# Post-norm block on one core: the later order of the maxima begins at step 20, with the quantizing in the middle of the step

## The chip, the cores and the metric

The kernel runs on one core of one Trainium2 chip. The metric is the device time of one execution in microseconds. The engines are TensorE (PE, with its weight loads as PEld), VectorE (DVE), ScalarE (ACT), GpSimd (POOL) and SyncE (SP), which here only issues DMAs.

## The reference, cut to what matters

For four sequences of 512 rows of width 512: attention with 16 heads of width 32 that share one key and one value head, rotary positions, a residual sum and a layer norm; then a gated feed-forward net with three weights that are first quantized to -1, 0 and 1, again a residual sum and a layer norm.

```python
q = rotary((x @ Wq + bq) by heads);  k = rotary(x @ Wk + bk);  v = x @ Wv + bv
attn = softmax(q @ k.T / sqrt(32));  ctx = attn @ v
x = layernorm(x + ctx @ Wo + bo)
quantize = lambda w: clip(round(w / (mean(abs(w)) + 1e-8)), -1, 1)
hidden = sigmoid(x @ quantize(w1).T) * (x @ quantize(w2).T)     # width 1408
x = layernorm(x + hidden @ quantize(w3).T)
```

## The kernel before, in words

**Steps.** The main loop (`for n, (b, c, t) in enumerate(steps)`, from line 865 on) has 64 steps: batch `b` of 4, group `c` of 4 heads, key chunk `t` of 4 (128 keys each). A step computes the scores of its four heads against its key chunk (`scores`: tiles `ps`, two exponentials `es`), and multiplies the previous step's exponentials with the values (`weigh`: `acc`). For batch 0 `count` also sums them into the PSUM bank `den`; for later batches POOL adds them up (`total`, four additions in each step but the first of a group), and `normalize` turns these into a divisor in several parts (`part`, `few`, `rden`).

**Maxima.** The scores need the row maxima beforehand. `find_maxima(n + 7, ...)` computes those of one head of a later group, seven steps ahead, in chunks of 128 queries: a matmul into `pmax` by PE and a reduce `maxima<-pmax` by DVE. `maximum` (line 379) says where `pmax` lies. PSUM has eight banks: two score buffers of two banks each (`ps_sc`), which the scores and the maxima use in turn, `acc` and `den` of one bank and one buffer each (`ps_acc`), and two buffers of one bank for all other products (`ps_mm`). A call with two chunks takes a score buffer. A call with one chunk takes `den` if it is chunk 0, or if `batches[-1].done == NC`, which is when the last batch's queries have been projected; otherwise a score buffer. With a head's last chunk in a group, `spread` (line 394) is entered in the list `late` three due times on: it transposes the group's maxima (`pm`, `m`) and sends them through DRAM (`rows`) into the tile `negm` that the scores take.

**Fill.** All other work of PE is cut into pieces and drawn between: `project_in` (keys, values and queries of a batch: `pk`, `pq`, with the rotation by four DVE operations), `project_out` (`po<-wo_sb`, then sum, statistics and layer norm on `xt`, then transposes `pt` and their two halves `y`), `feed_forward` (`gu`, `po<-wd`). `Fill.draw(us, least)` adds `us` to what is due and takes pieces, each counted at the length that it yields, while more than 0.9 is due; with `least` it takes one in any case. `Fill.one` changes between an urgent and an ordinary list. A step of batch 1 has a pace of 3.8. When nothing can be taken, what is due is set to zero.

**Due times.** `due` counts `slot` up, twice per step, and carries one part of each entry of `late` whose time has come (parts of `normalize`, `spread`, `layernorm`, storing of queries, and others).

**Quantizing.** `quantized` (line 158) has 66 jobs: three weights by eleven tiles, each tile read once for the mean and once to be quantized. A job of the second kind is a sign on ACT into `sgn`, a `scalar_tensor_tensor` on DVE (`raw<-raw,hi,sgn`), and two DMAs that POOL issues (`raw<-in_wf` for a later job, `w<-raw` for an earlier one). From step 17 on `sgn` lies in the tag `rot_a`, which has one buffer (line 210). 21 jobs are done ahead of step 0, two in each step of batch 0; from step 16 on one in each step and two where `n % 3 == 0`, so that the 66th falls in step 25. Steps 20 to 25 hold the last eight.

**Order.** `InOrder`, `mm`, `move` and `transpose` (lines 70 to 86) keep each engine's instructions in the order in which the program states them, so lines 75, 80, 83 and 86 stand for nearly all instructions in the profile, and tiles tell them apart. The order of a step of batch 1 is one of two, chosen at line 886. With the last batch not yet projected: maxima of chunk 0, of chunks 1 and 2, of chunk 3; first due time; one quantizing job; the whole draw; a second job where there is one; second due time. Otherwise: chunk 0; a draw of 0.4 of the pace; chunks 1 and 2; first due time; a draw of 0.3 with `least`; chunk 3; a draw of 0.3; second due time, and no quantizing.

Of the kernel before, what the change touches and what calls it, by code (L numbers as in the profile page):

```python
# [28 lines left out]
def postln_block(  # L29
# [17 lines left out]
    NC = D // P  # L47
    NT = T // P
# [30 lines left out]
    def mm(out, lhsT, rhs, start, stop):  # L79
        pin(nc.tensor.matmul(out, lhsT=lhsT, rhs=rhs, start=start, stop=stop))  # L80
# [36 lines left out]
    batches = [Batch() for _ in range(B)]  # L117

    chunks = iter([(b, c) for b in range(B) for c in range(NC)])
# [226 lines left out]
    def load_q(b, c):  # L346
        q = batches[b].q[c] = work.tile([P, T], F32, tag="qT", name="qT", bufs=3)
        move(q, batches[b].qd[c][0])
# [15 lines left out]
    def room_for_maxima(b, c):  # L364

        return maxima[c % 2][:, 0 : NG * NT].rearrange("p (i t) -> p i t", t=NT)
# [12 lines left out]
    def maximum(b, c, i, chunks, q):  # L379


        s = batches[b]
        if i == 0 and chunks[0] == 0:
            s.mx[c] = room_for_maxima(b, c)
        if len(chunks) == 1 and (chunks[0] == 0 or batches[-1].done == NC):
            ps = ps_acc.tile([P, 1, T], F32, tag="den", name="pmax")
        else:
            ps = ps_sc.tile([P, 2, T], F32, tag="sc", name="pmax")
        ps = ps[:, 0 : len(chunks), :]
        for n, t in enumerate(chunks):  # L390
            mm(ps[:, n, :], q[:, ts(t, P)], s.kr, True, True)
        dve.tensor_reduce(s.mx[c][:, i, chunks[0] : chunks[-1] + 1], ps, AX.X, ALU.max)
# [21 lines left out]
    def scores(b, c, t):  # L414
        s = batches[b]
        pss = []
        for j in range(2):
            ps = ps_sc.tile([P, 2, T], F32, tag="sc", name="ps")
            pss.append(ps)
            for i in range(2):  # L420
                rows = ts(2 * j + i, HD)
                mm(ps[:, i, :], s.kT[rows, ts(t, P)], s.q[c][rows, :], True, False)
        for j, ps in enumerate(pss):
            for i in range(2):
                rows = slice(HD * (2 * j + i), HD * (2 * j + i) + 2)
                mm(ps[:, i, :], ones_r[rows, :], s.negm[c][rows, :], False, True)
        es = []
        for j, ps in enumerate(pss):
            e = esp.tile([P, 2, T], F32, tag="es", name="es")
            act.activation(e, ps, AF.Exp, scale=SCALE)  # L430
            es.append(e)
        if b > 0:

            if t == 0:
                s.first = es
            elif t == 1:
                s.total = [work.tile([P, 2, T], F32, tag=f"total{j}", name="total", bufs=1) for j in range(2)]
                for j in range(2):
                    for i in range(2):
                        pool.tensor_tensor(  # L440
                            s.total[j][:, i, :], s.first[j][:, i, :], es[j][:, i, :], ALU.add
                        )
            else:
                for j in range(2):
                    for i in range(2):
                        pool.tensor_tensor(
                            s.total[j][:, i, :], s.total[j][:, i, :], es[j][:, i, :], ALU.add
                        )
        return es
# [5 lines left out]
    def weigh(b, c, t, es):  # L455
        s = batches[b]
        if t == 0:
            s.acc = ps_acc.tile([P, T], F32, tag="acc", name="acc")
            s.ctxT[c] = work.tile([P, T], F32, tag="ctxT", name="ctxT", bufs=6)
        columns(s.acc, s.v[:, t, :], es, t == 0, t == NT - 1)  # L460
        if t == NT - 1:
            act.copy(s.ctxT[c], s.acc)

    def count(b, c, t, es):

        s = batches[b]
        if t == 0:
            s.den = ps_acc.tile([P, T], F32, tag="den", name="den")
        columns(s.den, ones[:, 0:HD], es, t == 0, t == NT - 1)
# [95 lines left out]
    def load_x(b):  # L565
        batches[b].x = []
        for t in range(NT):
            xt = xp.tile([P, D], F32, tag="x", name="xt")
            move(xt, x[b, ts(t, P), :])
            batches[b].x.append(xt)  # L570
        yield
        for xt in batches[b].x:
            pool.tensor_tensor(xt, xt, bo_sb, ALU.add)
            yield
# [212 lines left out]
    def quantize(n):  # L787
        for _ in range(n):
            next(weights, None)

    steps = [(b, c, t) for b in range(B) for c in range(NC) for t in range(NT)]
    PER = NC * NT
# [5 lines left out]
    now = -1  # L798
# [3 lines left out]
    def due():  # L802

        nonlocal slot
        slot += 1
        for entry in list(late):
            if slot >= entry[0] and next(entry[1], "end") == "end":
                late.remove(entry)

    def begin_middle():  # L810
        late.extend(middle)
        middle.clear()
# [9 lines left out]
    def find_maxima(k, *chunks):  # L822

        if k >= len(steps):
            return
        b, c, i = steps[k]
        if chunks[0] == 0:
            ask(k + HEADS)
            while batches[b].done <= c or (b and k not in heads):
                if batches[b].done <= c:  # L830
                    fill.one()
                else:
                    begin_middle()
                    due()
                    ask(k)
        if b == 0:
            row_maxima(b, c, i, chunks[0] // 2)
        else:
            maximum(b, c, i, chunks, heads[k])
        if i == NG - 1 and chunks[-1] == NT - 1:  # L840

            late.insert(0, (slot + (1 if now < 0 else 3), spread(b, c)))

    def feed(b):
        fill.urgent.append(project_out(b))
        yield
# [18 lines left out]
    for n, (b, c, t) in enumerate(steps):  # L865
        now = n
        pace = (1.8, 3.8, 4.8, 4.6)[b]
        if t == 1 and PER <= n + NT - 1 < len(steps):
            load_q(*steps[n + NT - 1][:2])
        es = scores(b, c, t)  # L870
        if last is not None:
            weigh(*last)
        if last is not None and last[0] == 0:
            count(*last)
        last = (b, c, t, es)
        if n == NC * NT // 2:

            late.append((slot, load_x(0)))
        if t == NT - 1:
            begin = slot + 3  # L880
            late.append((begin, normalize(b, c)))
            if c == NC - 1:
                late.append((begin + 7, feed(b)))
                if b > 0:
                    late.append((slot + 6, load_x(b)))
        if batches[-1].done < NC:

            if b == 0:
                find_maxima(n + LEAD, 0, 1)
                begin_middle()  # L890
                due()
                find_maxima(n + LEAD, 2, 3)
            else:
                find_maxima(n + LEAD, 0)
                find_maxima(n + LEAD, 1, 2)
                find_maxima(n + LEAD, 3)
                begin_middle()
                due()
            quantize(1)
            fill.draw(pace)  # L900
            quantize(1 if b == 0 or n % 3 == 0 else 0)
        else:
            find_maxima(n + LEAD, 0)
            fill.draw(0.4 * pace)
            find_maxima(n + LEAD, 1, 2)
            begin_middle()
            due()
            fill.draw(0.3 * pace, True)
            find_maxima(n + LEAD, 3)
            fill.draw(0.3 * pace)  # L910
        due()
    weigh(*last)
    now = len(steps)
# [68 lines left out]
```

## Time and profile before

| what | value |
| --- | --- |
| median of 3 runs | 661.32 us (660.82 to 663.54) |
| the profiled execution | 659.87 us |
| its span, first to last instruction | 658.1 us |
| granted TensorE clock, mean | 0.997 |
| steps 20 to 25, by the starts of their scores | 179.94 to 223.97 us |
| DVE busy in steps 20 to 24 | 7.20 of 7.33, 7.35 of 7.42, 6.95 of 7.33, 6.66 of 7.32, 7.71 of 8.98 us |
| POOL busy in the same | 7.31, 6.64, 6.88, 6.54, 6.75 us |

A row of a timeline reads: start, length, engine, line, operation, tile written and tiles read, shapes, how many were merged into the row, and in brackets the idle time of the engine before it and what ended it. A `q` behind an engine's name is its queue of DMAs. A row of the windows reads: stretch, its length, busy time of each engine with the number of instructions, granted clock, share of the DMA engines, GB/s.

### The profile page before, as it was taken

What the parts mean: (1) busy time and instruction counts of PE and PEld (TensorE: products, weight loads), DVE (VectorE), ACT (ScalarE), POOL (GpSimd) and SP (SyncE); (2) the same over time, 40 slices, a digit from 0 to 9 for tenths busy, and PEclk for the clock granted to TensorE, in tenths of its full rate; (3) what the DMA queues carried; (4) which work ended last, traced back from release to release, by engine and by line L of the source; (5) the groups of instructions that cost most, each with busy time, mean ns of one, the idle gap of its engine ahead of it and who ended that gap; (6) DMA issues with size and microseconds to landing.
All of it is one profiled execution on the core that took longest, in us unless ns stands there. A gap on an engine that the chain in (4) does not pass through costs nothing.

```text
span 658.1 us, 9358 instructions
## 1 busy us (share of the span) xinstructions
PE 635.4 (97%) x3194; PEld 357.2 (54%) x3194; DVE 440.3 (67%) x629; ACT 282.6 (43%) x441; POOL 327.4 (50%) x416
## 2 busy tenths in 40 slices
PE   8999999999999999999999899999998999999995
PEld 5233333443333356665555566655555685778884
DVE  3987765787998977676666867667536544364335
ACT  2474656564454645333244354333454521234213
POOL 2434344545998766467666275576575703202000
PEclk9999999999999999999999999999999999999998
DMA  8946669788676286464132457541131473237531
GB/s 265 316 164 209 204 194 273 230 254 259 171 238 205 89 250 190 136 191 147 46 106 77 117 163 219 158 143 44 55 116 52 145 236 120 81 112 229 175 109 64
DMA packets 60671, 107.78 MB, mean 164 GB/s; under 512 B 14592, under 2 KB 15360, under 8 KB 60624
## 3 DMA queue, kind: packets, MB, share of 16 engines
q1 hardware_dynamic: 51984, 80.57, 40.2%
q0 software_dynamic: 7920, 25.96, 12.3%
q10 hardware_dynamic: 720, 0.66, 0.4%
q8 instruction: 25, 0.41, 0.3%
q14 instruction: 22, 0.18, 0.1%
HBM read 84.06 MB, written 23.10 MB: 163 GB/s over the span
## 4 chain that ended last, share of the span: by engine, by line
PE 85%; DVE 9%; ACT 4%; issue 2%; POOL 0%; DVEq 0%; ACTq 0%; POOLq 0%
PE gu L80 24%; PE po L80 19%; PE ps L80 13%; PE pmax L80 9%; PE acc L80 7%; PE pq L80 7%; DVE maxima L75 3%; ACT es L75 2%; PE den L80 2%; PE pk L80 2%; DVE part L75 1%; DVE xt L75 1%; DVE y L75 1%; DVE st L75 1%; PE warm L80 1%
## 5 line engine op out<-in xcount | busy, mean ns | idle before, releaser
L75 DVE TENSOR_REDUCE maxima<-pmax 128x1 f32<-128x512 f32 (+1 forms) x169 | 157.8, 955 | 69.9 <-PE pmax L80 69.7
L75 ACT ACTIVATE es<-ps 128x1024 f32<-128x1024 f32 x128 | 124.2, 1021 | 117.6 <-PE ps L80 116.7
L80 PE MATMUL gu<-y,wg 128*128 128x512 f32 x704 | 171.6, 393 | 0.1
L80 PEld LDWEIGHTS gu<-y,wg 128*128 128x128 f32 x704 | 131.7, 188 | 33.7 <-issue 4.9
L75 POOL TENSOR_TENSOR total<-total,es 128x512 f32<-128x512 f32 x96 | 125.2, 1336 | 38.5 <-ACT es L75 38.3
L80 PE MATMUL po<-wd,h 128*128 128x512 f32 x352 | 86.5, 394 | 3.3 <-DVE y L75 2.9
L75 POOL TENSOR_TENSOR total<-es 128x512 f32<-128x512 f32 x48 | 60.9, 1302 | 52.5 <-ACT es L75 52.5
L80 PE MATMUL pmax<-kr,qr 128*128 128x512 f32 x192 | 74.7, 452 | 3.2 <-DVE maxima L75 1.0
L80 PEld LDWEIGHTS po<-wd,h 128*128 128x128 f32 x352 | 65.1, 188 | 20.8 <-DVE y L75 4.6
L75 ACT CAST h<-hw 128x512 fp32r<-128x512 f32 x44 | 27.3, 620 | 103.0 <-DVE hw L75 103.0
L80 PE MATMUL acc<-es,v 128*32 128x512 f32 x512 | 68.2, 605 | 0.0
L80 PEld LDWEIGHTS pmax<-kr,qr 128*128 128x128 f32 x192 | 34.6, 188 | 55.9 <-issue 17.0
L75 DVE SCALAR_TENSOR_TENSOR hw<-th,gu 128x512 f32<-128x512 f32 x44 | 30.2, 686 | 44.3 <-PE gu L80 43.1
L80 PE MATMUL po<-wo_sb,ctxT 128*128 128x512 f32 x128 | 58.8, 592 | 0.0
L75 DVE TENSOR_TENSOR h<-hw,h 128x512 fp32r<-128x512 f32 x44 | 44.2, 1005 | 21.7 <-ACT h L75 21.4
L80 PE MATMUL ps<-negm,ones_r 2*128 2x512 f32 x256 | 58.7, 788 | 0.0
L75 DVE SCALAR_TENSOR_TENSOR xt<-po,xt 128x512 f32<-128x512 f32 x48 | 32.8, 684 | 37.0 <-PE po L80 37.0
L80 PE MATMUL ps<-qT,kT 32*128 32x512 f32 x384 | 56.3, 640 | 0.0
L75 POOL DMA_DIRECT2D raw<-in_wf x66 | 36.0, 548 | 38.1 <-DMA w<-raw 27.2
L80 PE MATMUL pq<-xT,wq_sb 128*128 128x512 f32 x112 | 53.1, 602 | 0.9 <-ACT v L75 0.9
L75 ACT ACTIVATE th<-gu 128x512 f32<-128x512 f32 x44 | 26.3, 597 | 49.9 <-PE gu L80 49.8
L80 PEld LDWEIGHTS po<-wo_sb,ctxT 128*128 128x128 f32 x128 | 24.1, 189 | 21.2 <-issue 19.2
(99 smaller groups left out, 640.2 us busy)
## 6 DMA issues: line engine op xcount, KB each, us to landing
wg<-w SPq DMA_DIRECT2D x88, 256.0 KB
raw<-in_wf POOLq DMA_DIRECT2D x66, 256.0 KB, 4.6
qr<-qp SPq DMA_DIRECT2D x96, 128.0 KB
wd<-w SPq DMA_DIRECT2D x44, 256.0 KB
w<-raw POOLq DMA_DIRECT2D x33, 256.0 KB, 4.6
qp<-q SPq DMA_DIRECT2D x48, 128.0 KB
rden<-flat SPq DMA_DIRECT2D x64, 64.0 KB
xt<-in_x SPq DMA_DIRECT2D x16, 256.0 KB
```

Source lines behind the costliest of these rows:

```text
L75: return lambda *args, **kw: pin(getattr(self.engine, name)(*args, **kw))
L80: pin(nc.tensor.matmul(out, lhsT=lhsT, rhs=rhs, start=start, stop=stop))
```

## The change

The condition that chooses between the two orders, and the one that sends a single chunk to `den`, become conditions on the step: below `PER + NT = 20` the first order, from step 20 on the second. In the second, one quantizing job, or two where `n % 3 == 0`, now stands behind the first due time.

```diff
@@ maximum @@
-        if len(chunks) == 1 and (chunks[0] == 0 or batches[-1].done == NC):
+        if len(chunks) == 1 and (chunks[0] == 0 or now >= PER + NT):
             ps = ps_acc.tile([P, 1, T], F32, tag="den", name="pmax")
         else:
             ps = ps_sc.tile([P, 2, T], F32, tag="sc", name="pmax")
@@ main loop @@
-        if batches[-1].done < NC:
+        if n < PER + NT:
 
             if b == 0:
                 find_maxima(n + LEAD, 0, 1)
...
             find_maxima(n + LEAD, 0)
             fill.draw(0.4 * pace)
             find_maxima(n + LEAD, 1, 2)
             begin_middle()
             due()
+            quantize(1 if n % 3 else 2)
             fill.draw(0.3 * pace, True)
             find_maxima(n + LEAD, 3)
             fill.draw(0.3 * pace)
         due()
```

## The prediction

> **What bounds the kernel now.** I call the value of `n` in the main loop the step, and the row maxima of one head's four chunks M0 (chunk 0), M12 (chunks 1 and 2) and M3 (chunk 3). First the page, for the whole; then the timeline of PE, where the shape of the maxima shows which order a step is in; then busy time per step, then DVE's timeline.
>
> ```profile
> PE 635.4 (97%) x3194; PEld 357.2 (54%) x3194; DVE 440.3 (67%) x629; ACT 282.6 (43%) x441; POOL 327.4 (50%) x416
> ...
> PE 85%; DVE 9%; ACT 4%; issue 2%; POOL 0%; DVEq 0%; ACTq 0%; POOLq 0%
> ```
>
> PE sets the end (span 658.1). The steps are counted off by their scores (`ps<-`); `den<-es`, which batch 0 alone writes, is last seen in step 16, from 149.43. Steps 20 to 27 then begin at 179.94, 187.27, 194.69, 202.02, 209.34, 218.32, 223.97 and 232.71. Up to step 25 all four maxima stand together; step 26 has M0, fill, M12, fill, M3. So the switch now comes at step 26, and **the change moves six steps, 20 to 25, 44.0 us of 658**. Step 22 on PE:
>
> ```profile
> 194.69 1.14 PE L80 MATMUL ps<-qT,kT 32*128 32x512 f32 x8
> ...
> 196.99 0.97 PE L80 MATMUL pmax<-kr,qr 128*128 128x512 f32 x3
> 198.15 0.50 PE L80 MATMUL pmax<-kr,qr 128*128 128x512 f32 x1 [0.19 <-ACT es L75]
> 198.49 3.59 PE L80 MATMUL po<-wo_sb,ctxT 128*128 128x512 f32 x8
> 202.02 1.14 PE L80 MATMUL ps<-qT,kT 32*128 32x512 f32 x8
> ```
>
> Its M0 begins 2.30 after the step does, M3 waits for an exponential (0.19), and the step lasts 7.33. Step 38 has the same pieces (two of `po<-wo_sb`, each half a product) in the later order, with no quantizing:
>
> ```profile
> 316.22 1.14 PE L80 MATMUL ps<-qT,kT 32*128 32x512 f32 x8
> ...
> 318.52 0.50 PE L80 MATMUL pmax<-kr,qr 128*128 128x512 f32 x1
> 318.86 1.88 PE L80 MATMUL po<-wo_sb,ctxT 128*128 128x512 f32 x4
> 320.18 1.03 PE L80 MATMUL pmax<-kr,qr 128*128 128x512 f32 x2
> 321.04 1.88 PE L80 MATMUL po<-wo_sb,ctxT 128*128 128x512 f32 x4
> 322.36 0.79 PE L80 MATMUL pmax<-kr,qr 128*128 128x512 f32 x1
> 323.08 1.14 PE L80 MATMUL ps<-qT,kT 32*128 32x512 f32 x8
> ```
>
> It lasts 6.86, so the order alone is worth 0.47 a step. But DVE was free in step 38 and is not here (columns: stretch, its length, busy PE, PEld, DVE, ACT, POOL):
>
> ```profile
> 194.69:202.02 7.33, 7.14 (x34) 2.79 (x33) 6.95 (x9) 3.27 (x4) 6.88 (x9) 1.00 0.84 275
> 316.22:323.08 6.86, 6.86 (x33) 2.86 (x33) 2.96 (x6) 2.68 (x4) 4.21 (x4) 1.00 0.03 7
> ```
>
> **The change part by part.** *Fill.* Pieces count 1.8 each against a pace of 3.8. Drawing at once, and drawing 0.4, 0.3 and 0.3 of it with the second draw forced, both take 2, 2, 2, 2, 3, 1 pieces in steps 20 to 25, and both end step 25 at zero; the work of PE is the same. In step 25 the first draw stands at 0.72, below 0.9, and takes nothing.
>
> *M3 in the bank `den`.* Taken away: one of four turns per step of the score banks, and the 0.19. Added: `den` has one buffer, so M3 waits for the reduce of M0, and the next step's M0 for the reduce of M3. Behind that M0 stand all of PE's pieces. The price of such a wait is in this trace, in step 49: the reduce of M3 runs 406.63 to 407.31, and PE says
>
> ```profile
> 407.36 0.50 PE L80 MATMUL pmax<-kr,qr 128*128 128x512 f32 x1 [0.65 <-DVE maxima L75]
> ```
>
> In step 38 the chain on DVE is M12 (321.24), its end 322.47, then 0.56 idle until the product is there, `xt` 323.03, statistics, M3's end 325.24; the next M0 starts 325.38. **The slack is 0.56 + 0.14 = 0.70 us**, before anything is put in.
>
> *The quantizing.* `scalar_tensor_tensor` on `raw` now stands between M12 and `xt`, inside that chain. Its rows:
>
> ```profile
> 196.81 0.75 DVE L75 SCALAR_TENSOR_TENSOR raw<-raw,hi,sgn 128x512 f32<-128x512 f32 x1
> ...
> 199.87 1.84 DVE L75 SCALAR_TENSOR_TENSOR raw<-raw,hi,sgn 128x512 f32<-128x512 f32 x1
> ```
>
> It takes 0.75 where POOL issues DMAs or nothing, and ends 0.55 after the running POOL addition where there is one (201.71 after 201.15; another, from 193.66, 195.34 after 194.79). I use both by where POOL stands. The Trainium skill, "SBUF — State Buffer", § Who interferes with whom, says that a DVE instruction with two SBUF inputs and a GpSimd one that reads SBUF exclude each other, the second waiting for the whole first: the trace agrees on the wait. By that rule the full 0.75 would follow the wait, at most 0.20 more in each of four blocked steps, and the sum would be at most 3.3 instead of 2.5.
>
> In steps 21 and 24 two jobs now stand one behind the other. `sgn` has one buffer, so the second sign (0.72 on ACT) starts when the first `raw` ends, as ACT's 195.38 does now; today three operations on `xt` cover it, afterwards nothing does: DVE idles 0.77 twice. The quantizing's POOL DMAs keep their place in POOL's order, since neither fill nor M3 puts anything there. `spread` of the heads finished in steps 20 and 24 comes half a step later (its due time is counted from M3), with its transpose, `m`, and SP's `rows` and `negm` transfers; it is needed four steps on, so I cost it at 0.
>
> *The walk.* Let X be the start of M0 on PE. From step 38: the reduce of M12 starts at X + 2.72, the product is ready at X + 4.51, the next step begins at X + 4.56 and its M0 is due 2.30 later, or 0.05 after the end of M3's reduce. On DVE, start to start: M12 1.14, `part` 1.16, `xt`, statistics and M3 2.22 to the end, rotation 2.80.
> - Step 20: X = 182.49 as now. M12 from 185.21, `part` from 186.35, `raw` behind POOL's `q` (ends 188.02) until 188.57, M3 ends 190.70. Next X = 190.75, due 189.35: stall 1.40.
> - Step 21: M12 from 193.47, `raw` 194.61 to 195.36 (POOL's sums just over), sign, `raw` to 196.88, M3 ends 199.00. The transpose `pm` adds 0.2. X = 199.05, due 197.81: 1.24.
> - Step 22: `raw` behind the last sum (203.04) to 203.60; M3 ends 205.76; X = 205.91, no stall.
> - Step 23: `raw` from 209.78 behind the third sum (209.9) to 210.45; M3 ends 212.6; X = 212.77, no stall. This is an edge: if the fourth sum goes first, +1.2.
> - Step 24: M12 from 215.49, `part`, `raw` behind POOL's `ctxT` product (over near 217.8) to 218.38, sign, `raw` to 219.9, rotation to 222.7, and only then M3, which ends 223.28. Step 25 begins at 219.10 (218.32 now); its X = 223.33, due 221.40: 1.93.
> - Step 25: `part`, M0, M12, `raw` from 226.05 behind the last sum (226.65) to 227.2, rotation to 230.0, M3 to 230.57; X = 230.62 against 226.67 now, due 228.70: 1.92.
> - Step 26 is gated now by the rotation (`pt` idles 1.13 for `q`, ended 229.14) and by four `y`; it ends 232.71. Afterwards M0, `pt` and the y's follow 230.62: the last `pt` at about 234.6, end 235.2.
>
> Stalls of 6.5 us (1.40 + 1.24 + 1.93 + 1.92) stand against 2.1 from six shorter steps (not 2.8, since step 20 begins as now and steps 24 and 25 have other pieces) and 1.9 that step 26 idles now and then has behind it: **2.5 us later at step 27** (235.2 - 232.7). From there PE's idle is some 6 us in 420, mostly local waits for `y`, so I let all of it reach the end: 659.87 + 2.5 = 662.4 for the profiled execution. The median of the runs shown is 661.32, 1.45 above it; with the same offset, **663.8 us**, +0.38%. About 0.5% (3.3 us) is what a measurement of this kernel can tell from no change.
>
> Bounds: with every `raw` at 0.75 the walk ends 1.7 later than now; with every one at 1.84, 10 later, which needs POOL in an addition at each of eight moments. I stay near the lower end because by the walk POOL is idle, issuing or ending at six of them.
>
> **Rivals.**
> - *The reduce of M3 is in time.* Then the six steps gain 2.1 and at most six times 0.47: 658.5 to 659.2. For it: step 38 runs so. Against: DVE is busy 6.95 of 7.33 here, and a slack of 0.70 is less than the cheapest `raw`, plus `part` and rotation. It decides where `raw` and what else is in the chain add under 0.7.
> - *POOL's sums come first.* The edge in step 23 is lost: +1.2, so +3.7, 665.0. It decides at 0.1 to 0.2 us of timing. For it: 199.87 lost with 0.06 to spare. More such losses: +5 to +8.
> - *`negm` is late.* `m` ends near 230.8 and step 28 needs `negm` near 241.4; two round trips (1.85, as from `flat` to `rden`, to 4.4 each) and 1.5 of issue fit with 0 to 5 to spare. Price up to 2 us: 666.
> - *Nothing moves*, if the switch came before step 20 already: 661.3. The order of the maxima in steps 20 to 25 speaks against it.
>
> **How the numbers follow.** Forecast 0.50 (663 to 664.5); M3 in time 0.08 (658 to 660); edge lost 0.27 (664.7 to 665.5); more POOL losses 0.10 (666 to 669); late `negm` 0.03; nothing 0.02. Faster by over 0.5% takes a little of the second, 0.03; slower is 0.27 + 0.10 + 0.03 = 0.40; within, 0.57. The range 660.0 to 667.0 leaves out most of the second case and the upper half of the fourth.
>
> **What would show it.** Right: in steps 20 to 25 M0 idle `<-DVE maxima` by over 1 us in steps 21, 22, 25 and 26 and not in 23; the 0.19 `<-ACT es` gone; DVE idle before the second `raw` of steps 21 and 24 `<-ACT sgn`; step 27 at about 235. Wrong: M0 without idle time (then the chain is shorter than I think), another number of pieces per step, scores waiting for `negm` in steps 24 or 28, or a delay at step 27 that the end doesn't show.

## The result and the profile after

The change makes the kernel slower by a third of a per cent: 664.55 us median (663.15 to 667.04, 22 runs) against 662.62 (660.71 to 664.94, 22 runs), ratio 1.0034, 95% interval 1.0023 to 1.0046, which is 1.5 to 3.0 us. The forecast was 1.0038 (663.8 over 661.32), or 2.5 us. It started from the median of three runs; that of 22 is 1.3 us higher, so the difference is to be compared, not 663.8. The profiled execution took 663.68 us against 659.87; of these 3.8 us, 1.01 stand ahead of step 20 (0.57 of it in step 17), where both kernels issue the same instructions, so the difference of two single profiles is no measure. I measure instead **the stretch from the start of step 20 to the start of step 28: 58.42 us before (179.94 to 238.36), 61.13 after (180.95 to 242.08), 2.71 more**. Behind it both need the same: 419.74 and 419.82 us.

The page of the changed kernel: PE does the same work in a longer span.

```profile
span 661.9 us, 9359 instructions
...
PE 635.2 (96%) x3194; PEld 358.1 (54%) x3194; DVE 436.8 (66%) x629; ACT 282.4 (43%) x441; POOL 327.2 (49%) x416
```

PE's timeline shows where, in steps 21, 22, 25 and 26:

```profile
191.54 0.50 PE L80 MATMUL pmax<-kr,qr 128*128 128x512 f32 x1 [1.37 <-DVE maxima L75]
...
199.87 0.50 PE L80 MATMUL pmax<-kr,qr 128*128 128x512 f32 x1 [1.28 <-DVE maxima L75]
...
224.33 1.65 PE L80 MATMUL pmax<-kr,qr 128*128 128x512 f32 x3 [2.12 <-DVE maxima L75]
225.77 2.82 PE L80 MATMUL pq<-xT,wq_sb 128*128 128x512 f32 x4
...
232.18 0.50 PE L80 MATMUL pmax<-kr,qr 128*128 128x512 f32 x1 [0.94 <-DVE maxima L75]
```

Each is M0 waiting for the bank `den`. DVE in step 21 shows the chain in which M3's reduce stands, with the second `raw` waiting for its sign; M3's reduce ends at 199.81, M0 begins 0.06 later:

```profile
194.26 1.23 DVE L75 TENSOR_REDUCE maxima<-pmax 128x2 f32<-128x1024 f32 x1 [1.04 <-PE pmax L80]
195.40 0.74 DVE L75 SCALAR_TENSOR_TENSOR raw<-raw,hi,sgn 128x512 f32<-128x512 f32 x1
196.94 0.75 DVE L75 SCALAR_TENSOR_TENSOR raw<-raw,hi,sgn 128x512 f32<-128x512 f32 x1 [0.79 <-ACT sgn L75]
197.61 0.68 DVE L75 TENSOR_TENSOR xt<-xt,po 128x512 f32<-128x512 f32 x1
...
199.15 0.66 DVE L75 TENSOR_REDUCE maxima<-pmax 128x1 f32<-128x512 f32 x1
```

The windows of steps 21, 23 and 25 (granted clock in the third column from the right) show a step with the wait, one without, and one in which the clock is not full:

```profile
187.81:196.22 8.41, 7.04 (x34) 3.00 (x34) 7.22 (x10) 2.58 (x4) 7.88 (x9) 1.00 0.95 305
204.42:211.27 6.85, 6.85 (x34) 2.87 (x33) 5.77 (x12) 2.55 (x3) 4.64 (x5) 1.00 0.41 129
219.84:228.86 9.02, 6.90 (x30) 3.12 (x29) 8.63 (x12) 6.02 (x9) 5.82 (x6) 0.81 0.26 92
```

Step 23 needs 6.85, as step 38 did (6.86); a step of this order is faster than one of the old (7.32) when nothing waits.

### The profile page after: what moved, and what is told of

Read it like the earlier page. It is cut to its first block, busy times and chain, and to the rows that moved or that the text cites. A ratio compares the mean times of both kernels' runs of the same rounds, so it can differ in the third digit from the quotient of the medians.

```text
span 661.9 us, 9359 instructions
## 1 busy us (share of the span) xinstructions
PE 635.2 (96%) x3194; PEld 358.1 (54%) x3194; DVE 436.8 (66%) x629; ACT 282.4 (43%) x441; POOL 327.2 (49%) x416
## 4 chain that ended last, share of the span: by engine, by line
PE 76%; DVE 10%; DMA 4%; SPq 3%; POOL 2%; issue 2%; ACT 2%; DVEq 0%; ACTq 0%; POOLq 0%
PE gu L80 24%; PE po L80 17%; PE ps L80 11%; PE pmax L80 8%; PE acc L80 7%; PE pq L80 5%; DVE maxima L75 3%; SPq L83 3%; PE den L80 2%; DMA xT<-in_xT 2%; PE pk L80 1%; DVE part L75 1%; POOL total L75 1%; DMA rows<-m 1%; DVE xt L75 1%
## 5 line engine op out<-in xcount | busy, mean ns | idle before, releaser
L80 PE MATMUL pmax<-kr,qr 128*128 128x512 f32 x192 | 79.9, 476 | 8.1 <-DVE maxima L75 6.7
L80 PE MATMUL po<-wo_sb,ctxT 128*128 128x512 f32 x128 | 59.5, 592 | 0.0
L80 PE MATMUL pq<-xT,wq_sb 128*128 128x512 f32 x112 | 54.3, 611 | 0.9 <-ACT v L75 0.9
```

## The experiments

Two theories. **CHAIN**: what stands on DVE between M12 and M3 delays M3's reduce, and through the one buffer of `den` PE. **LOAD**: DVE has too much to do in these steps, in whatever order. In what follows "stretch" is from step 20 to step 28, in one profile each, and a stall is the idle time of PE ahead of an instruction; ratios are to the kernel before, from 6 to 12 executions. Two of the runs, the other half of the switch and M3 in a score buffer, were executed once and have no ratio.

**Quantizing behind M3.**

```diff
-            quantize(1 if n % 3 else 2)
             fill.draw(0.3 * pace, True)
             find_maxima(n + LEAD, 3)
             fill.draw(0.3 * pace)
+            quantize(1 if n % 3 else 2)
```

> The changed kernel with the quantizing moved from the middle of the step to behind the third draw, so that on DVE it follows M3 instead of preceding it. Measure: the stretch from the start of step 20 to the start of step 28, 58.42 us in the profile of before and 61.13 in that of the change. Theory CHAIN (quantizing and other work between M12 and M3 makes M3's reduce late, and the one buffer of den hands that to the next step's M0): the stall of M0 in step 21 falls from 1.37 to about 0.4, that of step 22 from 1.28 to 0, that of step 25 from 2.12 to near 0; the stretch is 58.2 (57.9 to 58.8). Rival LOAD (DVE is simply full in these steps, the order of its work is of no matter): stalls elsewhere, stretch near 61. Rival ROTATION (only the rotation ahead of M3 in steps 24 and 25 costs): stalls of steps 21 and 22 as in the change, stretch about 60.

Stretch 60.82, ratio 1.0045 (1.0025 to 1.0066). Up to step 24 CHAIN is right: the stall of step 21 is 0.32, that of step 22 is gone, and steps 20 to 23 take 28.48 against 29.40 before and 30.32 in the change, although their five jobs are still in them, so LOAD is not what these steps lose by. From there it is wrong. Here are ACT and, below it, PE:

```profile
221.64 0.72 ACT L75 ACTIVATE sgn<-raw,hi 128x512 bf16<-128x512 f32 x1 [7.03 <-DVE raw L75]
222.27 1.50 ACT L75 ACTIVATE xt<-xt,ln 128x512 f32<-128x512 f32 x2
223.68 1.91 ACT L75 ACTIVATE es<-ps 128x1024 f32<-128x1024 f32 x2
```

```profile
224.73 0.50 PE L80 MATMUL pmax<-kr,qr 128*128 128x512 f32 x1 [3.18 <-ACT es L75]
```

The second sign of step 24 waits for the first `raw`, which now stands behind rotation and M3, and the next step's exponentials queue behind that sign on ACT. PE waits 3.18 us for them. Another 1.58 for weights (`wg`) follows in step 27, and behind the stretch the scores of step 28 wait 0.73 for `negm`: this is the rival "`negm` is late", met here. From step 28 to the end this profile takes 421.90, 2.1 more than the kernel before.

**M3 directly behind M12** in steps 20 to 25:

```diff
             find_maxima(n + LEAD, 1, 2)
+            if n < PER + NT + 6:
+                find_maxima(n + LEAD, 3)
             begin_middle()
...
-            find_maxima(n + LEAD, 3)
+            if n >= PER + NT + 6:
+                find_maxima(n + LEAD, 3)
```

> The changed kernel with M3 of steps 20 to 25 put directly behind M12, ahead of the due times, the quantizing and the second draw; the first draw still stands between M0 and M12. CHAIN: M3's reduce follows that of M12 at once, no M0 stalls for a maximum in steps 21 to 26, PE gains about 0.4 a step, and step 26 is gated by the rotation as before: stretch from step 20 to step 28 is 57.0 (56.0 to 58.4), the time 1 to 2 us below before. LOAD: stretch 60 or more. ROTATION: stalls of steps 21 and 22 stay, stretch about 60.

Stretch 60.76, ratio 1.0008 (0.9992 to 1.0024). Wrong again, by new waits. M0 waits for no maximum, but M3 does, in the other direction: it needs `den` from M0's reduce, and DVE reaches that late. In step 23 it is late for a transfer that DVE used to reach when it had landed. DVE, then PE:

```profile
205.99 0.60 DVE L75 TENSOR_REDUCE few<-few 32x64 f32<-32x256 f32 x1 [1.31 <-DMA few<-parts]
...
207.37 2.37 DVE L75 TENSOR_REDUCE maxima<-pmax 128x1 f32<-128x512 f32 x3
```

```profile
208.07 0.50 PE L80 MATMUL pmax<-kr,qr 128*128 128x512 f32 x1 [1.22 <-DVE maxima L75]
```

In step 25 M3 waits 2.26 for M0's reduce, which stands behind the rotation; the clock then falls (last section), and the piece behind it takes 3.58 us. The stretch of this profile is 2.34 longer than before, while the ten executions allow 1.6 at most (0.24%), so the profile is not typical of them; which part the others lack is not shown.

**The switch at step 24** (both conditions `PER + 2 * NT` in place of `PER + NT`), and **the other half**, the later order in steps 20 to 23 alone:

```diff
-        if len(chunks) == 1 and (chunks[0] == 0 or now >= PER + NT):
+        if len(chunks) == 1 and (chunks[0] == 0 or PER + NT <= now < PER + 2 * NT or now >= PER + NT + 6):
...
-        if n < PER + NT:
+        if n < PER + NT or PER + 2 * NT <= n < PER + NT + 6:
```

> The changed kernel with both conditions at step 24 instead of 20, so that steps 20 to 23 are as before. CHAIN: what steps 24 and 25 lose (two jobs with the wait for the sign, then the rotation, ahead of M3) stays, the stalls of steps 21 and 22 are gone; the change lost 0.92 up to step 24 and 1.79 from there to step 28, so the stretch from step 20 to step 28 is 60.2 (59.6 to 60.6). LOAD: steps 20 to 23 are as before, DVE is equally full, the loss falls by the share of the steps that are undone, stretch 58.8 to 59.5. If the quantizing between M12 and M3 in steps 20 to 23 made all of the loss: 58.4.

> The later order in steps 20 to 23 alone, steps 24 and 25 in the old order with their quantizing and M3 in a score buffer, from 26 the later one again: the other half beside the run with the switch at step 24. If the losses of the two halves are independent (0.92 up to step 24 in the change), the stretch from step 20 to step 28 is 59.3 (59.0 to 59.8). If the old order in steps 24 and 25 takes the lateness of DVE in (LOAD says that it does not): 58.4. If both halves are needed for the loss: 58.4 too, with the half that was run before at 58.4, which it was not (60.31).

The switch at step 24: stretch 60.31, as CHAIN said, ratio 1.0017 (1.0001 to 1.0034); stalls of 2.17 and 2.42 in steps 25 and 26. The other half: 60.28, not 59.3, with stalls of 1.72 and 1.27 in steps 21 and 22. So each half has a loss of its own (1.89 and 1.86), more together than the 2.71 of the change. Step by step the second half is nearly the same in both: steps 24 to 27 lose 1.90 with the switch at step 24 and 1.79 in the change. The first half is not: steps 20 to 23, the same instructions, lost 1.51 here and 0.92 in the change. Of these 0.59, 0.27 stand in step 20 ahead of M0; most of the rest has a reason on DVE: `raw` of step 20 took 1.45 here and 1.10 there, by where POOL's addition stood. The other 0.35 of the 1.86 is in step 27, where PE waits 0.48 for weights (`wg`), which it does neither before nor in the change. With the 0.92 of the change the two halves add up to 2.82: in these profiles they are nearly independent.

The 0.27 matters for every comparison of stretches. M0 of step 20 begins 2.55 to 2.59 after its step in the seven other profiles with the same instructions ahead of step 20, the kernel before among them, and 2.30 in that of the change. So the stretch of the change from the usual state would be some 0.3 longer if nothing else moved; this is an estimate from these starts.

**Two buffers for the sign:**

```diff
-                    sgn = work.tile([P, W], BF16, tag="rot_a", name="sgn", bufs=1)
+                    sgn = work.tile([P, W], BF16, tag="th", name="sgn")
```

> The changed kernel with sgn of the quantizing in a tag of two buffers, so that the second sign of steps 21 and 24 need not wait for the first raw. CHAIN: DVE's idle time of 0.79 ahead of the second raw is gone in both steps; the stall of step 22 falls from 1.28 to about 0.5 and that of step 25 from 2.12 to about 1.3; the stretch from step 20 to step 28 falls by 0.8 to 1.6, to 59.5 to 60.3. LOAD: DVE idles elsewhere instead, 61.1. If ACT is too late in any case (its exponentials come first): idle time stays, 61.1.

Stretch 61.12, where 59.5 to 60.3 was expected, ratio 1.0024 (1.0001 to 1.0046): no gain. The idle time ahead of the second `raw` is gone and the stall of step 22 is 0.40, as expected. Then DVE is earlier in its step, and meets POOL's sums in their middle. DVE of this run:

```profile
202.60 1.52 DVE L75 SCALAR_TENSOR_TENSOR raw<-raw,hi,sgn 128x512 f32<-128x512 f32 x1
...
210.14 1.30 DVE L75 SCALAR_TENSOR_TENSOR raw<-raw,hi,sgn 128x512 f32<-128x512 f32 x1
```

In the change the same two took 0.74 and 0.76; the one of step 25 took 1.70 instead of 1.45. So most of what the buffer gave went into waits of DVE for POOL, with new stalls of 0.62 and 0.41 in steps 23 and 24. This is the rival "POOL's sums come first", met here and not in the change. What was left, the clock took: counted from the start of step 20, M0 of step 26 begins 0.33 earlier than in the change, behind a stall of 2.56, but step 26 then runs at half clock and step 27 begins no earlier. (Step 20 is 0.28 longer here than in the change, as said above of the seven.)

**M3 in a score buffer** in steps 20 to 25 (`now >= PER + NT + 6` in the condition of `maximum`).

> The changed kernel with M3 of steps 20 to 25 in a score buffer as before, everything else as in the change. The second pair of the next step's scores then waits for M3's reduce, some 1.9 us earlier in the step than M0 does with den. CHAIN: stalls are longer by up to 1.9 in each of steps 21, 22, 25 and 26, part of it made up by DVE idling less: stretch from step 20 to step 28 63 to 66. If the bank den were the cost of the change: 59 or less. If the bank is of no matter: 61.1.

Stretch 89.81, 28.7 more than the change, where I had expected 2 to 5. The direction is CHAIN's: the scores themselves now wait, 2.58, 2.51, 1.09, 1.09, 3.32 and 2.18 us in steps 21 to 26, 12.8 together. The size is the clock's, as the windows of steps 21, 22 and 25 show:

```profile
187.63:199.92 12.29, 9.71 (x35) 3.92 (x34) 7.31 (x10) 2.58 (x4) 8.23 (x10) 0.86 0.81 253
199.92:213.63 13.71, 11.20 (x33) 4.15 (x32) 5.51 (x10) 3.38 (x5) 6.80 (x8) 0.75 0.36 105
...
238.35:252.09 13.74, 10.42 (x30) 3.97 (x30) 8.92 (x12) 6.09 (x9) 6.04 (x5) 0.63 0.08 24
```

Over steps 20 to 26 PE is busy 70.6 us for work that took it 49.6 before, at a granted clock between 0.63 and 0.86; idle time grew from 3.2 to 14.0. So `den` is not the cost of the change; in this one execution the change without it is far worse.

**The quantizing out of these steps.** Eight more jobs in steps 4 to 11, with the later order and with the old one:

```diff
-            quantize(1 if b == 0 or n % 3 == 0 else 0)
+            quantize(2 if 4 <= n < 12 else 1 if b == 0 or n % 3 == 0 else 0)
```

> The changed kernel with one more quantizing job in each of steps 4 to 11, so that the last eight jobs are done before step 20 and steps 20 to 25 hold none. Measure: the stretch from the start of step 20 to that of step 28, 58.42 us before, 61.13 in the change. CHAIN and LOAD together say: without the eight jobs the stall of step 21 falls to about 0.4, those of steps 22 and 25 go, the rotation in step 25 alone delays step 26; stretch 55.4 (55.0 to 57.0). What eight jobs more cost in steps 4 to 11 is 0 to 1.5. If quantizing were no part of the loss: 61. Time against before: -3 to -1.

> The kernel before (the switch when the last batch is projected, step 26) with the same earlier quantizing, so that steps 20 to 25 have the old order and no jobs. LOAD: DVE gets free, the rotation in step 25 ends about 2 earlier, and PE's idle time of 1.13 for it in step 26 goes: stretch 56.4 (55.9 to 57.0), 1 us more than with the later order, since each step keeps the 0.19 and the ends of four maxima in a row. If the old order has no use for a free DVE: 58.4.

Stretches 54.98 and 56.37. With the later order PE keeps two of its four stalls. These are its M0 of steps 21, 22 and 26; in step 25 it has no stall either:

```profile
202.03 0.50 PE L80 MATMUL pmax<-kr,qr 128*128 128x512 f32 x1 [0.32 <-DVE maxima L75]
...
209.01 0.50 PE L80 MATMUL pmax<-kr,qr 128*128 128x512 f32 x1
...
237.56 0.51 PE L80 MATMUL pmax<-kr,qr 128*128 128x512 f32 x1 [0.94 <-DVE maxima L75]
```

Four stretches, two by two:

| | eight jobs in steps 20 to 25 | done before step 20 |
| --- | --- | --- |
| old order up to step 25 | 58.42 | 56.37 |
| later order from step 20 | 61.13 | 54.98 |

**This settles the cause.** The later order is worth 1.39 us where DVE has room, and costs 2.71 where the quantizing stands in it. The eight jobs cost 2.05 in the old order and 6.15 in the later one; the 4.10 between is the collision. The stretch without them and with the later order came out at 54.97 to 55.02 in three more runs (below). Of the stalls only 0.32 in step 21 (`part`) and 0.94 in step 26 (rotation) stay. The table takes sign, `raw` and transfers away together; that the place of `raw` in DVE's order counts is what the run with the quantizing behind M3 shows, for steps 20 to 23.

As whole kernels both are slower (ratios 1.0109, 1.0066 to 1.0151, and 1.0161, 1.0115 to 1.0206): the additional jobs were expected to cost 0 to 1.5 and cost more. With the later order steps 11 and 12 lose 9.4 us: POOL, which issues the loads of the quantizing, stands 10.3 us behind an addition that waits for `x`, ACT waits for tiles (up to 4.0 us), and the clock falls for two windows. With the old order these two steps lose 6.0, and step 16, where the scores wait 3.37 for `negm`, another 6.3.

**Looking for a version that beats both.** The same eight jobs in steps 0 to 7; eight ahead of step 0 (the expectation says nine, but one five and six fours instead of seven threes are eight more); and spread around POOL's standstill, without and with M3 of step 25 placed early:

```diff
+            quantize(2 if n < NT * 2 else 1 if b == 0 or n % 3 == 0 else 0)
...
+        quantize(5 if n == 0 else 4)
...
+            quantize(2 if n < 8 or 12 <= n < 15 else 0 if 9 <= n < 12 else 1 if b == 0 or n % 3 == 0 else 0)
```

> The changed kernel with the eight additional jobs in steps 0 to 7 instead of 4 to 11 (from step 9 to 12 POOL's queue, which issues the loads of the quantizing, stands still for 10 us behind an addition that waits for x, and three jobs a step ran out of loaded tiles there). Stretch from step 20 to step 28 55.0 (54.9 to 55.8), as in the run with steps 4 to 11 (54.98), against 58.42 before. If only that standstill cost the 10 us, steps 0 to 19 lose 0 to 2 and the whole is 1 to 3 us below before. If three jobs a step are too many for the DMA queues in any place, steps 0 to 19 lose 5 or more and the whole is slower.

> The changed kernel with nine additional jobs ahead of step 0 (four instead of three beside each of the seven first heads, five beside the first), so that the last job falls before step 20. Stretch from step 20 to step 28 55.0 (54.9 to 55.8). Ahead of step 0 the transfers of the inputs run beside them; if they have room the whole is 1 to 3 us below before, if ACT waits there for loaded tiles as it does for the ninth tile in before (2.2 us) the start is up to 6 later and the whole up to 3 above.

> The changed kernel with three quantizing jobs a step in steps 0 to 7 and 12 to 14, two in step 8, one in each of steps 9 to 11, where POOL's queue stands behind the addition that waits for x, and as in the change from 15 on, so that the 66th job falls before step 20. Stretch from step 20 to step 28 55.0 (54.9 to 55.5). The run with the additional jobs in steps 0 to 7 alone lost 4.26 us up to step 20, 1.7 of it in step 0 and about 2.1 in steps 10 to 15; if these 2.1 come from jobs that find no tile loaded in steps 10 and 11, they go, and the whole is 2 to 4 below before; if they come from more jobs altogether, the time is that run's, ratio to before 0.998.

> The same as q_spread, with M3 of step 25 ahead of the due times and the second draw, so that its reduce stands before the rotation on DVE. CHAIN: M0 of step 26 no longer waits for it (0.94 us now), the rotation ends 0.6 sooner and gates the transposes of step 26 alone: stretch from step 20 to step 28 54.3 (54.0 to 55.0). If the four y's of step 26 bound it in any case: 55.0.

| version | stretch | start of step 20 | ratio to before |
| --- | --- | --- | --- |
| before | 58.42 | 179.94 | 1 |
| in steps 0 to 7 | 55.02 | 184.20 | 0.9979 (0.9957 to 1.0002) |
| ahead of step 0 | 54.98 | 189.27 | 1.0086 (1.0053 to 1.0120) |
| spread | 54.97 | 184.47 | 0.9992 (0.9973 to 1.0010) |
| spread, M3 early in step 25 | 55.30 | 184.01 | 0.9996 (0.9978 to 1.0013) |

The stretch is the expected 55.0 in the first three (54.3 was expected of the last), and the start of step 20 takes it back; behind step 28 these profiles need another 0.6 to 1.2 more than before. Of the 4.26 by which the first is late at step 20, 1.71 are a fall of the clock in step 0 (last section). The one with the jobs ahead of step 0 is 9.33 late where up to 6 was expected; 5.68 of it stand in step 0, which runs at half clock for three windows. That POOL's standstill was the only price is refuted: in the spread version POOL's addition waits 0.4 instead of 10.3, no clock falls, and it is 4.5 late at step 20 all the same. Why the jobs cost that much there was not pursued. Three of the four are faster than the change (the intervals don't meet). The first is faster than before by a hair that its interval doesn't exclude to be nothing. Early M3 in step 25 moved the wait from M0 of step 26 to M3 itself (0.71).

## Why the prediction was right, point by point

- *Which steps, which order, how many pieces*: right. Every step draws the pieces counted beforehand.
- *The walk*, for M0's start and with the 1.01 us taken off that the profile is late before step 20:

| step | predicted start of M0 | measured - 1.01 | predicted stall | measured |
| --- | --- | --- | --- | --- |
| 21 | 190.75 | 190.53 | 1.40 | 1.37 |
| 22 | 199.05 | 198.86 | 1.24 | 1.28 |
| 23 | 205.91 | 205.70 | 0 | 0 |
| 24 | 212.77 | 212.55 | 0 | 0 |
| 25 | 223.33 | 223.32 | 1.93 | 2.12 |
| 26 | 230.62 | 231.17 | 1.92 | 0.94 |

- *Step 20*: its M0 was put at 2.55 after its start, as before, and stood at 2.30 in this profile (see the switch at step 24 and its other half): the walk met a state 0.25 better than it assumed.
- *The sign's wait*: 0.77 twice predicted, 0.79 twice measured. *The edge in step 23*: `raw` went first (0.76), and POOL's fourth sum stretched to 1.72. Of the two prices of a blocked `raw`, the row's was right for steps 20 (1.10, against 1.07 in the walk and 1.3 by the rule weighed there) and 25: 1.45, ending 0.55 after POOL's sum at 228.05.
- *Step 25 and 26, mis-sized twice.* `raw` of step 25 was put down to end 0.55 after a sum at 226.65. The sum came later: POOL's third sum waited 0.58 for DVE's `part`, which reads the tile that it overwrites. I had let POOL run through:

```profile
225.57 2.48 POOL L75 TENSOR_TENSOR total<-es 128x512 f32<-128x512 f32 x2 [0.58 <-DVE part L75]
```

And the stall in step 26 is 0.94 instead of 1.92, though M0 is 0.55 later than foreseen, because PE reached it 1.5 later: step 25 ran partly at half clock (below). That cost next to nothing at the end, since M0 waited for DVE: the rotation began at 228.63, when `raw` (228.60) and the piece on PE (228.59) had both just ended. That these two ended together is luck: had PE been later still, the rotation would have begun later.
- *At step 27* 2.5 was predicted and 3.1 measured; step 27 gave 0.4 back, which the prediction did not count, which leaves 2.7 at step 28, and the rest carried it to the end unchanged, as assumed. So the mechanism and the four steps with a stall are right. That the sum is right to 0.2 is in part luck: M0 of step 26 came 0.55 later than predicted, and step 27 gave most of that back.
- *`negm`*: no scores wait for it in the change, right; with the quantizing behind M3 they do (0.73 in step 28).
- *The rivals.* "M3 in time" needs a chain without quantizing; the runs that had one kept 0.32 in step 21 and 0.94 in step 26. The interval of the bounds (1.7 to 10) held. That the edge could be lost was shown by the run with two sign buffers.
- What the prediction did not see, and the runs did: that each single repair (order on DVE, position of M3, another buffer) only hands the wait on, to ACT's queue, to `den` in the other direction, to a transfer, or to POOL. CHAIN is right as the mechanism of the stalls; as a recipe it is not enough, and LOAD alone is not either, since the later order is the faster one without the load.

## What to carry to other kernels

Before an order is moved into a stretch, ask what the engine that frees its single buffers has to do there, and price the chain from one use of the buffer to the next in that stretch, not in the one where the order was seen to be good: 0.70 us of slack were used up by one operation of 0.75. Steps 22 and 23, which had that alone in the chain, handed no stall on; steps 20, 21, 24 and 25, which had `part`, a second job or the rotation beside it, did. If two changes are in one edit, run the two by two table; here the order gained 1.39 by itself and the quantizing cost 2.05, and their collision cost 4.10 more. And a wait that is repaired by itself in a full stretch is handed on; the work has to leave the stretch, and where it goes it is paid again.

## What the runs showed of the hardware

**The clock falls by windows, after less idle time than I thought safe.** In the change PE was idle from 222.20 to 224.33 and the granted clock went to 0.5 from 224.25 to 227.67, 3.42 us; the piece `pq` at 225.77 (four matmuls) took 2.26 us to the next matmul, where 1.31 is usual. All half-clock stretches of the runs last 3.41 us or a multiple of it, but for the one in which each program ends, and within a trace all changes of the granted clock stand whole such windows apart. Counting in windows of 3.41 us from the falls, every window with 2.05 us or more of idle PE was followed by one at half clock: 2.05 in the change, 2.26 with M3 behind M12, 2.42 with the switch at step 24, 2.56 with two sign buffers, 2.51 with M3 in a score buffer. What counts is the idle time inside one window: a wait of 3.18 with the quantizing behind M3 lay across two (1.37 and 1.80) and made no fall, nor did one of 2.17 with the switch at step 24 (1.85 in one). Below that idle time alone does not decide: in several runs falls followed windows with 0.95 to 1.6 us idle, with M3 in a score buffer and in step 0 above all, while others with as much were followed by none; what else counts there the runs don't show. The Trainium skill, "TensorE: Matmul & The Clock Gate", § What's actually happening, has the free-running window of 3.4 us, which these runs confirm, but a whole idle window as the condition for the fall; here 60% of one was enough, and the measurement decides. Part of the noise between profiles is such falls: in five of the thirteen that were taken after the first, one stands at 48.8 to 49.5 us, in step 0, and step 1 then begins some 1.7 us later for it. The window ahead of it held 1.08 to 1.09 us of idle PE, and as much in three profiles without a fall.

**The exclusion of DVE and POOL is a matter of phase.** In steps 20 to 25 of these runs the same `raw` operation took 0.71 to 1.84 us (ahead of them up to 3.22). Where it met a POOL addition with 0.19 us or more left there, it ended 0.54 to 0.56 us after it; in the kernel before the one from 199.87 met the last 0.06 of an addition, and ended 0.55 after the next. So timing decides: with two sign buffers DVE reached `raw` of step 22 0.63 us earlier in the stretch than in the change, and the operation took 1.52 instead of 0.74.
